# Second dense layers of a four-layer graph network with features on partitions

## The chip, the cores and the metric

The kernel runs on one core of a Trainium2 chip. The metric is the device time in microseconds of one execution. The kernel before takes 2306.15 us, the median of three runs between 2304.9 and 2306.2.

## The reference

32 graphs of 512 nodes with 256 features each pass through four layers. Every layer multiplies by the graph's own dense 512x512 adjacency matrix, adds the layer's input and normalises over the features. All arithmetic is float32.

```python
x = layernorm(x + relu(((1 + eps) * x + adj @ x) @ W1 + b1) @ W2 + b2)      # layer 0, hidden 512
h = adj @ (x @ W.T + b);  x = layernorm(x + where(h > 0, h, alpha * h))     # layer 1
h = layernorm(x);  x = layernorm(x + relu((adj @ h) @ W_rel + b_rel + h @ W_root) + x)   # layer 2
h = silu(rmsnorm((eps * x + adj @ x) @ W1 + b1))                            # layer 3, hidden 1024
x = layernorm(x + h @ W2 + b2)
```

(In layer 2 the layer's own result already contains x once.)

## The kernel before, in words

A graph is held as x in "token" layout: 128 partitions, on each of them four nodes (chunks c) with 256 features. SBUF has 36 buffers of 4 KB a partition ("rooms", line 639), PSUM its 8 banks, and there are 11 small tiles (`SMALL`, line 612).

Each large product is done with seven block products in place of eight (Strassen's scheme in Winograd's form). `seven` (line 764) calls `product` for m1 to m7 on three banks, and `take` or `put` to bring a bank into SBUF; `right_sums` and `weight_sums` make the sums of blocks that the seven products need. `aggregate` (line 880) gives adj @ x with features on partitions. `dense_feat` (line 920) is the first dense layer: weights are the stationary operand, 256 nodes the moving one, and hidden features stand on partitions. `dense_add` (line 963) is the second dense layer: nodes are the stationary operand, 128 columns of weights the moving one, and the product comes out in token layout. All seven `take` and `put` there are VectorE additions of a bank and a block of x, 128x256 elements. The bias of layers 0 and 3 has been added to x before, by `plus_row` (line 1138), two VectorE additions of 128x512. `done(j)` then starts the sums of the norm for half of the nodes.

Layer 2 needs its input with features on partitions too. `turned` (line 1092) does this in graphs 0 and 31 (`alone()`, line 628) with TensorE transposes, and in the others with two VectorE transposes, which turn each 32x32 square in place, and sixteen transfers within SBUF (`carry`) that put the squares where they belong.

The norm is class `Norm` (line 1015). It sums on ScalarE, one pass for the mean and one for the squares. `NormOnVector` (line 1079) takes VectorE's statistics. `layer3` (line 1219) uses the latter in graphs 0 and 31. The last graph (`b == B - 1`) ends its norm by halves of the nodes and stores each half (`finish`, line 1049); others are scaled and stored whole.

No engine's order is that of the program text. Every operation is recorded first (`Plan.add`), with the engines that can do it and an estimated duration. `order` (line 423) then plays the program through: at each step it takes the engine and operation that can start earliest, and among those that can start at about the same time the lowest rank. The rank is the graph's number times `period`, plus the TensorE work of its graph ahead of the operation times `pace`; the last three graphs (`LATE`) are spaced by `last` in place of `period`. `FLIGHT` allows five graphs at once, and rooms are kept back for older graphs. An operation that ScalarE or VectorE can do goes to VectorE only where this ends earlier by more than `YIELD`. `best` (line 417) plays each of the `RULES` and takes the one whose last operation starts earliest. The engines then get this order, fixed; each works through its own list and waits for the others through semaphores. All transfers are issued by SyncE, whose list is in the same order. Where GpSimd's power and a VectorE operation would meet, short VectorE memsets (`pause`, line 1316) keep them apart.

Of the kernel before, what the change touches and what calls it, by code (L numbers as in the profile page):

```python
# [14 lines left out]
P = 128  # L15
Q = 32
# [15 lines left out]
def matmul_time(n):  # L32
    return (0.224 if n <= 128 else 0.432), 0.163
# [47 lines left out]

TWO_OPERANDS = ("tensor_add", "tensor_sub", "tensor_mul", "scalar_tensor_tensor")
PORT = 0.55

# [1 line left out]
SOON = 0.03  # L88


YIELD = 0.8

# [2 lines left out]

RULES = [(48, 2, 8, 0.7), (48, 2, 20, 0.5), (45, 2, 12, 0.7)]  # L100

AHEAD, LAST = 70.0, 500.0


class Pool:
# [62 lines left out]
class Part:  # L170
# [10 lines left out]
    def __getitem__(self, i):  # L181
        return self.then(lambda v: v[i])

    def shaped(self, *shape):

        n = 1
        for d in shape:
            n *= d
        names = "abcd"[: len(shape)]
        kw = dict(zip(names, shape))  # L190
        return self.then(
            lambda v: v[:, 0:n].rearrange(f"p ({' '.join(names)}) -> p {' '.join(names)}", **kw)
        )
# [38 lines left out]
class Plan:  # L232
# [190 lines left out]
    def order(self, period, pace, last, near):  # L423

        final = max(op.graph for op in self.ops) - LATE
        need = self.needs(pace, near)
        rank = [
            (min(op.graph, final) * period + max(op.graph - final, 0) * last + n, i)
            for i, (op, n) in enumerate(zip(self.ops, need))
        ]  # L430
        tensor = sorted(r for r, op in zip(rank, self.ops) if "tensor" in op.ways)
# [14 lines left out]
        port = dict.fromkeys(free, 0.0)  # L446
        powers = {i for i, op in enumerate(self.ops) if op.port and "gpsimd" in op.ways}
        can_start = {i for i, n in enumerate(behind) if not n}
        crossed = False
        done = []  # L450
        while can_start:
            while oldest in left and not left[oldest]:
# [71 lines left out]
            op = self.ops[i]  # L524
            op.start, op.way = t, engine
            busy, tail = op.ways[engine][0]
            if engine == "tensor" and t > free[engine] + 0.01:
                busy += AGAIN
            if engine == "vector":
                crossed = op.crosses  # L530
                if crossed:
# [43 lines left out]
def tile_gnn_stack(ctx: ExitStack, tc: tile.TileContext, a: dict, out: bass.AP):  # L575
# [33 lines left out]
    HC = NC // 2  # L609
    TH = N // 2  # L610
    FH = FC3 // 2
    FLIGHT, ROOMS, SMALL = 5, 36, 11

    const = ctx.enter_context(tc.tile_pool(name="const", bufs=1))
    work = ctx.enter_context(tc.tile_pool(name="work", bufs=1))
# [6 lines left out]
        [  # L622
            memory.tile([P, 2, 2, P], F32, tag=f"diagonal{i}", name=f"diagonal{i}")
            for i in range(FLIGHT)
        ]
    )

# [15 lines left out]
    def vector(method, n, *args, **kw):  # L643
        return "vector", method, vector_time(n), args, kw
# [4 lines left out]

    def mm(o, lhsT, rhs, first, last):  # L650
        kw = dict(start=first, stop=last, skip_group_check=True)
        way = "tensor", "matmul", matmul_time(rhs.shape[-1]), (lhsT, rhs), kw
        plan.do(o, way, ordered=o.room)

    def flip(o, x):
# [29 lines left out]
    def carry(o, x):  # L685
        plan.move(o, x, o.shape[0] * span(o) / 256, late=1.2)
# [11 lines left out]
    def short(*shape):  # L698
        return Part(Room(rooms, whole=False)).shaped(*shape)
# [4 lines left out]
    def bank(*shape):  # L704
        return Part(Room(banks)).shaped(*shape)
# [22 lines left out]
    def constant(name, shape):  # L728
        return const.tile(shape, F32, tag=name, name=name)
# [27 lines left out]
    nc.vector.memset(scraps[0], 0.0)  # L757
    nc.vector.memset(mhalf, -0.5)
    pause = constant("pause", [P, 48])
    for tile_of_few in smalls.tiles:  # L760
        nc.vector.memset(tile_of_few, 0.0)

# [27 lines left out]
    def right_sums(b11, b12, b21, b22, t, t3):  # L790

        sub(t[0], b12, b11)
        sub(t[1], b22, t[0])
        sub(t3, b22, b12)
        sub(t[2], b21, t[1])
        return dict(m1=b11, m2=b21, m3=b22, m4=t[2], m5=t[0], m6=t[1], m7=t3)
# [123 lines left out]
    def dense_feat(aT, left, bias, hT, done):  # L920
# [6 lines left out]
        for f0 in range(0, n, 2):  # L927
# [21 lines left out]

            seven(*(bank(2, TH) for _ in range(3)), product, take, put)  # L950

    def dense_sums(upper, lower):


        right = {}
        for pairs in zip(upper, lower):
            blocks = [x[:, :, j * TH : (j + 1) * TH] for x in pairs for j in range(2)]
            sums = right_sums(*blocks, [short(2, TH) for _ in range(3)], blocks[1])
            for m, x in sums.items():
                right.setdefault(m, []).extend(x[:, e, :] for e in range(2))  # L960
        return right

    def dense_add(x, right, left, done):


        def block(i, j):
            return x[:, j * HC : (j + 1) * HC, i * P : (i + 1) * P]

        def product(m, ps, first):
            n = len(right[m])  # L970
            for k in range(n):
                for i in range(HC):
                    mm(
                        ps[:, i, :], right[m][k][:, i * P : (i + 1) * P], left[m][:, k, :],
                        first and i == 0 and k == 0, k == n - 1,
                    )

        def take(ps, i, j):
            add(block(i, j), ps, block(i, j))

        def put(ps, i, j, more):
            take(ps, i, j)
            if i == 1:
                done(j)

        seven(*(bank(HC, P) for _ in range(3)), product, take, put)

    def column_sums(t):

# [99 lines left out]
            ts(self.less[:, mine], means[:, mine, 0], -1.0, None, ALU.mult)  # L1089
            self.squares, self.n = means[:, :, 1], 1  # L1090

    def turned(h):

        hT = Wide(DC)
        if alone():
            for k in range(DC):
                ps = bank(N)
                for c in range(NC):
                    flip(ps[:, c * P : (c + 1) * P], h[:, c, k * P : (k + 1) * P])
                copy(hT.chunk(k), ps)  # L1100
        else:
            squares = Wide(DC)
            for k in range(DC):
                o = squares.chunk(k)
                plan.do(o, vector("transpose", N, h[:, :, k * P : (k + 1) * P]))
            places = [slice(q * Q, (q + 1) * Q) for q in range(P // Q)]
            to, of = (
                x.pair(0).then(lambda v: v.rearrange("p k (c i) -> p (k c) i", i=P))
                for x in (hT, squares)
            )  # L1110
            for p in places:
                for q in places:
                    carry(to[p, :, q], of[q, :, p])
        return hT

    def everywhere(sums, ops):

# [47 lines left out]
    def layer0(x, adjacency):  # L1165
        adjacency.sums()
        adjacency.with_loops(loop0)
        aT = aggregate(x, adjacency)
        adjacency.restore()
        plus_row(x, b2_0)  # L1170
        h1 = Wide(FC0)
        dense_feat(aT, A1_0, b1_0, h1, lambda f: act(h1.pair(f), h1.pair(f), AF.Relu))
        norm = Norm(x)
        dense_add(x, dense_sums(h1.rooms[:1], h1.rooms[1:]), A2_0, norm.half)
        norm.scales((1.0, LN_EPS))
        return norm.scaled()

# [26 lines left out]
    def layer2(h, xx, u, adjacency):  # L1204

        aT = aggregate(h, adjacency)
        hT = turned(h)
        norm = Norm(xx)

        def done(h):  # L1210
            stt(half(xx, h), half(u, h), 0.0, half(xx, h), ALU.max, ALU.add)
            norm.half(h)

        dense_add(u, dense_sums(hT.rooms, [aT]), A_2, done)
        adjacency.with_loops(loop3)
        norm.scales((1.0, LN_EPS))
        return norm.scaled()

    def layer3(x, adjacency, b):

        aT = aggregate(x, adjacency)
        plus_row(x, b2_3)
        hT, acc = Wide(FC3), short(N)

        def squares(f):
            sq = room(2, N)
            act(sq, hT.pair(f), AF.Square)
            if f == 0:
                add(acc, sq[:, 0, :], sq[:, 1, :])
            else:  # L1230
                add(acc, acc, sq[:, 0, :])
                add(acc, acc, sq[:, 1, :])

        dense_feat(aT, A1_3, b1_3, hT, squares)
        pr = everywhere(column_sums(acc), (1.0 / HID3, RMS_EPS, ALU.mult, ALU.add))
        right = {}
        for q in range(0, FH, 2):
            for f in (q, q + 1, FH + q, FH + q + 1):
                mul(hT.chunk(f), hT.chunk(f), pr)
                act(hT.chunk(f), hT.chunk(f), AF.Silu, scale=w_3[:, f : f + 1])  # L1240
            for m, t in dense_sums([hT.pair(q)], [hT.pair(FH + q)]).items():
                right[m] = right.get(m, []) + t
        norm = (NormOnVector if alone() else Norm)(x)
        place = out[b].rearrange("(p c) d -> p c d", c=NC)
        if b < B - 1:
            dense_add(x, right, A2_3, norm.half)
            norm.scales((1.0, LN_EPS))
            y = norm.scaled()
            plan.move(place, y, N * D / 256, into=f"out{b}")
        else:  # L1250

            def done(h):
                norm.half(h)
                norm.finish(h, 1.0, LN_EPS, half(place, h))

            dense_add(x, right, A2_3, done)
# [17 lines left out]
    A1_0 = weight_sums("A1_0", *quarters(W1_0))  # L1274
    b1_0 = col("L0_gnn_b1")
    b2_0 = row("L0_gnn_b2")
    W2_0 = weight("L0_gnn_W2")
    A2_0 = weight_sums("A2_0", *blocks_of(W2_0[:, 0:2], W2_0[:, 2:]))
    alpha = row("L1_gnn_alpha")
# [17 lines left out]
    b1_3 = col("L3_gnn_b1")  # L1297
    w_3 = col("L3_gnn_rms_weight")
    b2_3 = row("L3_gnn_b2")
    eps3 = row("L3_gnn_epsilon")  # L1300
    loop3 = constant("loop3", [P, P])
    ts(loop3, ident, eps3, None, ALU.mult)
# [52 lines left out]
```

## Time and profile before

| | |
|---|---|
| median of three runs | 2306.15 us |
| the profiled execution | 2307.14 us, its span 2305.4 us |
| TensorE busy | 2286.7 us, 99% |
| weight loads busy | 2094.1 us, 91% |
| VectorE busy | 2167.7 us, 94% |
| ScalarE busy | 1583.2 us, 69% |
| GpSimd busy | 239.7 us, 10% |
| moved by DMA | 122.84 MB, 53 GB/s |

Busy is the time in which an engine runs at least one instruction. TensorE's matmuls overlap one another, so its busy time says that it has work, and not how fast this passes; the time from one start to the next says that. The chain is the work that ended last, followed back from the end. Almost every instruction has line 317 (the helper that issues), so groups are told apart by the tiles that they write and read: `ps` is a PSUM bank, `room` an SBUF buffer, `A` sums of weights, `L_gnn_W` weights, `few` a small tile, `line` and `diagonal` memory in DRAM.

### The profile page before, as it was taken

What the parts mean: (1) busy time and instruction counts of PE and PEld (TensorE: products, weight loads), DVE (VectorE), ACT (ScalarE), POOL (GpSimd) and SP (SyncE); (2) the same over time, 40 slices, a digit from 0 to 9 for tenths busy, and PEclk for the clock granted to TensorE, in tenths of its full rate; (3) what the DMA queues carried; (4) which work ended last, traced back from release to release, by engine and by line L of the source; (5) the groups of instructions that cost most, each with busy time, mean ns of one, the idle gap of its engine ahead of it and who ended that gap; (6) DMA issues with size and microseconds to landing.
All of it is one profiled execution on the core that took longest, in us unless ns stands there. A gap on an engine that the chain in (4) does not pass through costs nothing.

```text
span 2305.4 us, 41217 instructions
## 1 busy us (share of the span) xinstructions
PE 2286.7 (99%) x14002; PEld 2094.1 (91%) x14002; DVE 2167.7 (94%) x5556; ACT 1583.2 (69%) x4338; POOL 239.7 (10%) x167
## 2 busy tenths in 40 slices
PE   9999999999999999999999999999999999999998
PEld 8899999999999999999999999999999999999888
DVE  8999999999999999999999999999999999979898
ACT  4766767667677677676676766767767767676576
POOL 0001110111010111101111011110011110111101
PEclk9999999999999999999999999999999999999999
DMA  6112221122211222121221112221222212201101
GB/s 190 46 41 64 53 68 24 51 65 61 53 31 55 61 64 59 26 55 57 65 60 35 49 52 64 60 60 24 56 60 65 60 24 55 70 10 38 51 6 42
DMA packets 223747, 122.84 MB, mean 53 GB/s; under 512 B 142896, under 2 KB 194352, under 8 KB 223536
## 3 DMA queue, kind: packets, MB, share of 16 engines
q1 hardware_dynamic: 223536, 120.20, 19.2%
q8 instruction: 111, 1.82, 0.3%
q14 instruction: 100, 0.82, 0.1%
HBM read 78.92 MB, written 24.97 MB: 45 GB/s over the span
## 4 chain that ended last, share of the span: by engine, by line
PE 95%; DVE 2%; ACT 1%; DMA 1%; SPq 0%; issue 0%; ACTq 0%; DVEq 0%
PE ps L317 95%; DVE room L317 2%; ACT room L317 1%; DMA room<-in_adj_dram 1%; ACT scrap L317 0%; DMA L_gnn_W<-in_L_gnn_W_dram 0%; SPq L357 0%; DMA room<-line 0%; DVE few L317 0%; DVE few L336 0%; DVE A L317 0%; DVE pause L1316 0%; DVE L_gnn_W_root L317 0%; DVE L_gnn_W L317 0%; DVE L_gnn_W_rel L317 0%
## 5 line engine op out<-in xcount | busy, mean ns | idle before, releaser
L317 PE MATMUL ps<-room,room 128*128 128x256 f32 x3584 | 908.8, 381 | 1.6 <-DVE room L317 0.8
L317 DVE TENSOR_TENSOR room<-room,room 128x512 f32<-128x512 f32 (+1 forms) x1360 | 772.4, 595 | 14.6 <-ACT room L317 8.2
L317 PEld LDWEIGHTS ps<-room,room 128*128 128x128 f32 x3584 | 639.9, 191 | 75.6 <-DVE room L317 5.6
L317 DVE TENSOR_TENSOR room<-ps,room 128x256 f32<-128x256 f32 (+1 forms) x1344 | 611.2, 473 | 60.3 <-PE ps L317 42.9
L317 PE MATMUL ps<-L_gnn_W,room 128*128 128x128 f32 (+1 forms) x3584 | 600.6, 290 | 1.3 <-ACT room L317 0.8
L317 PEld LDWEIGHTS ps<-L_gnn_W,room 128*128 128x128 f32 x3584 | 525.7, 191 | 32.7 <-ACT room L317 1.8
L317 PE MATMUL ps<-A,room 128*128 128x128 f32 x3072 | 457.9, 275 | 0.0
L317 POOL TENSOR_TENSOR few<-few,mhalf 128x4 f32<-128x4 f32 (+3 forms) x161 | 239.0, 1485 | 2060.0 <-DVE few L317 1944.3
L317 PEld LDWEIGHTS ps<-A,room 128*128 128x128 f32 x3072 | 426.5, 191 | 18.9 <-DVE room L317 0.4
L317 PE MATMUL ps<-room,L_gnn_W 128*128 128x256 f32 x1536 | 400.4, 379 | 1.9 <-DVE room L317 1.9
L317 ACT ACTIVATE room<-ps,L_gnn_b_c 128x256 f32<-128x256 f32 x768 | 318.2, 475 | 70.9 <-PE ps L317 67.1
L317 ACT ACTIVATE room<-ps 128x256 f32<-128x256 f32 x509 | 186.4, 383 | 252.1 <-PE ps L317 248.9
L317 ACT ACTIVATE room<-room 128x1024 f32<-128x1024 f32 (+2 forms) x260 | 242.3, 944 | 132.6 <-DVE room L317 86.5
L317 ACT ACTIVATE scrap<-room 128x256 f32<-128x256 f32 x504 | 206.5, 411 | 170.2 <-DVE room L317 141.2
L317 PEld LDWEIGHTS ps<-room,L_gnn_W 128*128 128x128 f32 x1536 | 282.7, 190 | 38.5 <-DVE room L317 2.8
L317 DVE TENSOR_TENSOR room<-room 128x256 f32<-128x256 f32 (+1 forms) x640 | 311.7, 495 | 5.3 <-ACT room L317 2.1
L317 ACT ACTIVATE room<-room,few 128x256 f32<-128x256 f32 x525 | 286.4, 593 | 33.4 <-DVE few L317 33.3
L317 PE MATMUL ps<-room,A 128*128 128x256 f32 x1152 | 305.6, 381 | 3.0 <-ACT room L317 3.0
L317 ACT ACTIVATE scrap<-room,few 128x256 f32<-128x256 f32 x504 | 251.2, 502 | 20.1 <-DVE few L317 19.0
L317 PEld LDWEIGHTS ps<-room,A 128*128 128x128 f32 x1152 | 209.9, 191 | 31.7 <-ACT room L317 3.9
L317 ACT ACTIVATE room<-room,L_gnn_rms_weight_c 128x512 f32<-128x512 f32 x256 | 176.0, 714 | 33.2 <-DVE room L317 33.0
L317 DVE TENSOR_TENSOR room<-room,loop 128x256 f32<-128x256 f32 x256 | 103.8, 416 | 18.3 <-PE ps L317 15.8
(59 smaller groups left out, 1198.7 us busy)
## 6 DMA issues: line engine op xcount, KB each, us to landing
room<-in_adj_dram SPq DMA_DIRECT2D x128, 256.0 KB, 5.0
room<-in_x_dram SPq DMA_DIRECT2D x31, 512.0 KB, 5.9
out_dram<-room SPq DMA_DIRECT2D x31, 512.0 KB, 2.9
room<-room SPq DMA_DIRECT2D x480, 32.0 KB, 2.0
diagonal<-room SPq DMA_DIRECT2D x62, 128.0 KB, 1.8
room<-in_adj_dram SPq DMA_DIRECT2D x124, 64.0 KB, 2.0
room<-diagonal SPq DMA_DIRECT2D x62, 128.0 KB, 2.3
room<-line SPq DMA_DIRECT2D x30, 256.0 KB, 3.3
```

The costliest lines, as they stand in the source:

```text
L317: getattr(getattr(self.nc, engine), method)(to, *(put(x) for x in args), **kw)
```

## The change

1. `dense_turned` takes the place of `dense_add` in layers 0 and 3 of graphs 1 to 28 (`TURN`). Weights are now the stationary operand and 256 nodes the moving one, so features stand on partitions. Four of the seven results are brought to SBUF by ScalarE, which adds the bias; three are VectorE additions. Two VectorE transposes turn the 32x32 squares, `spread_squares` writes them to DRAM in four transfers and reads them back in one, and `add_turned` adds the result to x by halves. `plus_row` is left out there.
2. In layer 2 the sixteen transfers of `turned` become four into DRAM and four back (`gather_squares`). `dense_add` itself stays in layer 2, and in layers 0 and 3 of graphs 0 and 29 to 31.
3. The last two graphs (`HALVES`) take VectorE's statistics in the final norm, and end and store it by halves.
4. The planner has one rule (37, 2, 19, 0.6) in place of three, shifts for the ranks of the set-up, of graph 1 and of the last two graphs, `YIELD` 1.2 for 0.8, `AHEAD` 50 for 70, and a model of a TensorE that runs at half speed for a while after an idle time (`COLD`). `SMALL` is 10.
5. A Silu of one column ahead of all work makes ScalarE load its table then. Two bias columns are loaded besides.

```diff
-RULES = [(48, 2, 8, 0.7), (48, 2, 20, 0.5), (45, 2, 12, 0.7)]
-AHEAD, LAST = 70.0, 500.0
+RULES = [(37, 2, 19, 0.6)]
+SHIFT = {-1: -12, -2: 6, 1: -6}
+AHEAD, LAST = 50.0, 500.0
+TURN = {0: (0, 3), 2: (99, 0), 3: (0, 3)}
+HALVES = 2
...
+                if idle > COLD[0]:
+                    cold = t + COLD[1]
+                if cold - COLD[2] < t < cold:
+                    busy *= 2
...
-    FLIGHT, ROOMS, SMALL = 5, 36, 11
+    FLIGHT, ROOMS, SMALL = 5, 36, 10
...
+    nc.scalar.activation(pause[:, 0:1], pause[:, 0:1], AF.Silu)
...
+    def turns(layer):
+        return TURN[layer][0] < plan.graph < B - TURN[layer][1]
...
+    def dense_turned(right, left, bias=None):
+        yT = Wide(DC)
+        def product(m, ps, first):
+            n = len(right[m])
+            ps = ps.then(lambda v: v.rearrange("p (c a j) -> p c a j", c=HC, j=Q))
+            for k in range(n):
+                mm(ps, left[m][:, k, :], right[m][k], first and k == 0, k == n - 1)
+        def block(i, j):
+            return yT.chunk(i)[:, j * TH : (j + 1) * TH]
+        def take(ps, i, j):
+            if bias is None:
+                copy(block(i, j), ps)
+            else:
+                act(block(i, j), ps, AF.Identity, bias=bias[:, i : i + 1])
+        def put(ps, i, j, more):
+            if more:
+                add(block(i, j), ps, block(i, j))
+            else:
+                take(ps, i, j)
+        seven(*(bank(TH) for _ in range(3)), product, take, put)
+        squares = room(P // Q, NC, DC, Q)
+        for k in range(DC):
+            plan.do(
+                squares.then(lambda v: v.rearrange("p b c k j -> p k c b j"))[:, k],
+                vector(
+                    "transpose", N,
+                    yT.chunk(k).then(lambda v: v.rearrange("p (c b j) -> p c b j", c=NC, j=Q)),
+                ),
+            )
+        y = spread_squares(squares)
+        return y.whole(P // Q, NC, DC, Q).then(lambda v: v.rearrange("p a c k j -> p c k a j"))
+
+    def add_turned(x, y, done):
+        x = x.then(lambda v: v.rearrange("p c (k a j) -> p c k a j", k=DC, j=Q))
+        for h in range(2):
+            add(half(x, h), half(x, h), half(y, h))
+            done(h)
...
+    def spread_squares(of):
+        to = room(P // Q, NC * DC * Q)
+        of, via = of.whole(P // Q, NC * DC * Q), next(corners)
+        names = [f"{via.tensor.name}{a}" for a in range(P // Q)]
+        places = via.rearrange("(b i) (a x) -> a i b x", i=Q, a=P // Q)
+        for a, name in enumerate(names):
+            plan.move(places[a], of[a * Q : (a + 1) * Q], Q * N * DC / 256, into=name)
+        plan.move(to.whole(N * DC), via, P * N * DC / 256, late=0.8, outof=names)
+        return to
+
+    def gather_squares(to, of):
+        to, of, via = to.whole(N * DC), of.whole(N * DC // Q, Q), next(corners)
+        names = [f"{via.tensor.name}{a}" for a in range(P // Q)]
+        via = via.rearrange("(i b) x -> i (b x)", i=Q)
+        places = via.rearrange("i (m a j) -> a i m j", a=P // Q, j=Q)
+        for a, name in enumerate(names):
+            plan.move(places[a], of[a * Q : (a + 1) * Q], Q * N * DC / 256, into=name)
+        blocks = via.rearrange("i (b x) -> b i x", b=P // Q)
+        for b in range(P // Q):
+            plan.move(to[b * Q : (b + 1) * Q], blocks[b], Q * N * DC / 256, late=0.8, outof=names)
...
+        if turn:
+            add_turned(x, dense_turned(right, A2_0, b2c_0), norm.half)
+        else:
+            dense_add(x, right, A2_0, norm.half)
...
-        norm = (NormOnVector if alone() else Norm)(x)
+        norm = (NormOnVector if b == 0 or b >= B - HALVES else Norm)(x)
-        if b < B - 1:
-            dense_add(x, right, A2_3, norm.half)
+        if b < B - HALVES:
+            if turn:
+                add_turned(x, dense_turned(right, A2_3, b2c_3), norm.half)
+            else:
+                dense_add(x, right, A2_3, norm.half)
```

## The prediction

> **What bounds the kernel now.** I read the busy line and the chain of the page first, then the chain in order of time, then the busy times by stretch, then the instructions of TensorE (PE) in order of time.
>
> ```profile
> PE 2286.7 (99%) x14002; PEld 2094.1 (91%) x14002; DVE 2167.7 (94%) x5556; ACT 1583.2 (69%) x4338; POOL 239.7 (10%) x167
> ...
> PE 95%; DVE 2%; ACT 1%; DMA 1%; SPq 0%; issue 0%; ACTq 0%; DVEq 0%
> ```
>
> PE is busy for 99% of the span and makes up 95% of the chain that ended last. VectorE (DVE) is close behind, so both must be watched. A busy PE is not yet a PE at its rate, hence the next two views: the chain in time (start, length), and the stretch from 500 to 1000 us (length, then busy time and instructions of PE, weight loads, DVE, ACT, POOL, then clock, DMA share, GB/s).
>
> ```profile
> 62.35 2010.53 PE ps L317 x12322
> ```
>
> ```profile
> 500.00:1000.00 500.00, 500.00 (x3078) 458.66 (x3078) 474.25 (x1208) 347.46 (x963) 54.26 (x36) 1.00 0.20 53
> ```
>
> From 62 to 2073 us the chain is one unbroken piece of PE. In the stretch PE never idles at full clock, DVE is busy 474.25 of 500 (95%), ACT 347.5 (69%). What does one matmul instruction cost there? Each f32 product of the program stands in the trace as two MATMUL records ("passes"). Start to start in the timeline:
>
> ```profile
> 1031.68 2.75 PE L317 MATMUL ps<-room,room 128*128 128x256 f32 x12
> 1034.28 1.03 PE L317 MATMUL ps<-room,L_gnn_W 128*128 128x256 f32 x4
> 1035.14 1.03 PE L317 MATMUL ps<-room,A 128*128 128x256 f32 x4
> ...
> 2267.07 4.18 PE L317 MATMUL ps<-L_gnn_W,room 128*128 128x128 f32 x36
> ...
> 2271.09 0.61 PE L317 MATMUL ps<-A,room 128*128 128x128 f32 x4
> ```
>
> Twelve passes of 256 columns take 1034.28 - 1031.68 = 2.60 us, 0.2167 each; four of the first dense layer 0.86 us, 0.215 each. Thirty-six of 128 columns take 4.02 us, 0.1117 each. Over all starts between 100 and 2050 us the means are 0.1115 (128) and 0.2160 (256, first dense layers) to 0.2173 (256, aggregations). A graph has 106 products of 256 columns and 112 of 128: 212 x 0.2162 + 224 x 0.1115 = 70.8 us. The saved diagonals show the real period:
>
> ```profile
> 1004.46 0.96 SPq L357 DMA_DIRECT2D diagonal<-room  x2
> ...
> 1075.34 0.96 SPq L357 DMA_DIRECT2D diagonal<-room  x2
> ```
>
> 1075.34 - 1004.46 = 70.88 us. So in the middle only the number and width of the matmuls count; some 4 us in 2010 are anything else. The ends are different. Where each stretch is set against its passes at these rates, PE loses 8.9 us until its first product, 5.6 us from there to 62 us, 7.7 us from 2073 to 2293 us, and runs out of work at 2295.7, 9.7 us ahead of the end.
>
> **What the skill says of it.** The Trainium skill, page TensorE: Matmul & The Clock Gate, section Back-to-back issue gap, gives a matmul N/2.4 + 2.5 ns: a fixed part for each instruction, so that one wide one is cheaper than two narrow ones. The trace agrees in kind. If a f32 pass of N columns counts as 2N, the rule gives 109.2 and 215.8 ns, the trace 111.5 and 216.0. The saving for two passes made one is 2.5 ns by the rule and 7.0 by the trace; the forecast goes by the trace, because the change lives on just this difference. For the transfers, DMA: Bandwidth & Descriptors, Specifications, asks for at least 512 B in a piece. The trace has 142896 packets under 512 B, and the 32 KB transfers that are made of them land after 2.0 us, as late as a 128 KB diagonal (1.8). The new transfers of layers 0 and 3 have pieces of 1 KB and 4 KB; I price them by the diagonal and line rows.
>
> **The change part by part**, against the profiled execution (2307.1 us, span 2305.4).
>
> *Matmuls, layers 0 and 3.* 28 + 56 products of 128 columns become 14 + 28 of 256. Per graph 42 x (4 x 0.1115 - 2 x 0.2160) = 42 x 0.014 = 0.59 us. This holds in graphs 1 to 28 (layer 2 stays): 28 x 0.59 = 16.5 us, all of it on the path. Bounds: with 0.2173 for the wide pass 14.3 us at least, with a rounded 0.112 19 at most. Weight loads halve there; they were behind PE anyway.
>
> *DVE, per turned layer.* Gone: two row additions of the bias (684 ns) and four of seven additions out of PSUM (416 ns), 3.03 us. New: two transposes of 128x512 (690) and two additions of 128x512 (682), 2.74 us. So -0.29 us, twice a graph: 67.2 becomes 66.7 us in a period of 70.3, 95% as before. The new operands come in runs of 32 elements. No row has just these; steps of 4 elements (158 ns for 32x4) and diagonal blocks of 128 (416 ns, as contiguous ones) cost nothing extra, so I take none. The upper bound, twice the time, would be 5.5 us a graph and is in the rivals.
>
> *ACT.* Four evictions with bias at 475 ns per turned layer: +3.8 us on about 49 per graph, 76% of the period. ACT's longest waits are for PE already, and that free time covers them; were it gone, a bank would come free half a us later and PE would wait for it. The higher penalty for vector (1.2 for 0.8) moves some of the 115 scalings at 406 ns from DVE to ACT (593). Both nothing on the path.
>
> *Transfers.* Per turned layer four writes of 128 KB (about 0.45 us issue each, landing 1.8 as the diagonal) and a read of 512 KB. The line row has 256 KB in 3.3 us, the prefetched x 512 KB in 5.9; I take 4 to 5. With transposes and issues the sum is 10 us of latency, twice a graph. It lies beside other graphs' matmuls. The addition of y is what waits; behind it on DVE, which works in order, are other graphs' evictions, and PE waits for their banks. Layer 2's sixteen transfers (about 0.65 us issue each, 10.4 in sum) become four and four, some 8 us for 12. SyncE has then 34 issues for 32 a graph, with waits for writes in between; adjacency and x loads queue behind these, but land well ahead of use now. Bytes go from 3.5 to 6 MB a graph, the DMA share from 0.20 to some 0.3. I charge 0.8 us in all; bounds 0 and the rival below.
>
> *End.* The last graph's final norm is as before. The one before takes DVE statistics (four of 406 and four of 174 ns, 2.3 us, in DVE's idle time there) and halves in place of eight ACT sums and their reads:
>
> ```profile
> 2299.55 1.01 ACT room L317 x2
> ...
> 2300.61 0.60 ACT room L317
> 2301.20 0.49 ACTq L1351
> ```
>
> That graph's last store goes out at 2301.7, the last graph's own at 2300.7; with the former early the end follows the latter: -1.1 us. The new ranks (period 37 and 19 at the end, shifts, half clock in the planner's costs) can save part of the 7.7 us lost from 2073 on, of which 3 is this wait and some 2.5 the half clock after it:
>
> ```profile
> 2204.91 1.72 PE L317 MATMUL ps<-room,A 128*128 128x256 f32 x4 [2.98 <-ACT room L317]
> ```
>
> It can also add as much, since more graphs meet at the end. Bounds -7.7 and +8; I take -3.0.
>
> *Start.* The table load (1.28 us at 5.10) goes ahead of the first data, where ACT idles. DVE waited 1.3 us for the copies behind it, but PE's first product waited for x, which lands at 8.8. I take -0.7, bounds -2 and +2. One small buffer of eleven fewer costs nothing: the waits show none for these. Two small bias columns add about 1 us of SyncE issue, covered by loads under way.
>
> Sum: -16.5 + 0.8 - 1.1 - 3.0 - 0.7 = -20.5 us, 2286.6 in the profiled execution's terms. The median of the runs is 1.0 lower than that execution: 2285.6.
>
> **Rivals.**
> 1. *The gain is half eaten.* A turned layer holds up to a room more until its transposes, and 36 rooms with about 3.8 graphs under way (2 x 71 / 37) are fewer than ten each; loads or banks come late and PE idles 0.2 to 0.5 us a graph, or the ends get 5 to 8 us worse. 2285.6 + 7 to 17: 2292 to 2303. For: DVE has only 5% free. Against: 4 us of loss in 2010 now.
> 2. *Slower: DVE is stopped by the addition of y.* If y lands later than the order written ahead of time allows, DVE stands at that addition. Its free time is 70.3 - 66.7 = 3.6 us a graph. From there on each us is PE's, and above 3.6 + 0.73 us (20.5 / 28) the change loses. At 5.5 us, 2.7 for each of two waits: 1.9 x 28 = 53 us, about 2339. Runs of 32 at double time come to the same. For: in-order engine, no margin seen for a 512 KB read. Against: DVE waited just 1.4 us in all for the line transfers, which are of this kind.
> 3. *The change does nothing in the middle*: a turned pass costs 0.2195 and the wide form saves nothing beyond 4 x 0.1115 - 2 x 0.2195 = 0.007, half. Then 2294, inside rival 1. The first dense layers at 0.2160 speak against it.
>
> **How the numbers follow.** The main case has 0.66, its own range 2277 to 2293; rivals 1 and 3 together 0.23; rival 2 0.11, reaching from 2306 to 2345. The likeliest gives 2285.6. A range from 2277 to 2301 leaves out rival 2, the upper edge of rival 1 and a little below. A measurement of this kernel can tell about 0.2%, 4.6 us, from no change: faster (below 2301.5) 0.66 + 0.19 = 0.85, within 0.04, slower 0.11.
>
> **What would show it.** Right: a period of 70.3 us between the saved diagonals; twice as many ACT evictions with bias less some; PE without idle time in the middle; DVE near 95%. Wrong: DVE or PE waits on a transfer named room<-corner, passes of a turned layer above 0.216, or PE idle beyond 16 us at the ends.

## The result and the profile after

The kernel takes 2336.89 us after the change (median of 4 runs, 2330.42 to 2340.77) and 2306.18 before, on the same chip. The ratio is 1.0131, 95% interval 1.0118 to 1.0143: the change costs 30.7 us, where I had forecast a gain of 20.5. The profiled execution is 2338.3 us, its span 2336.5.

The page first, its busy line and the chain that ended last by engine:

```profile
PE 2283.9 (98%) x11650; PEld 2014.7 (86%) x11650; DVE 2134.7 (91%) x5390; ACT 1696.2 (73%) x4600; POOL 239.7 (10%) x168
...
PE 29%; DVE 3%; DMA 3%; ACT 1%; issue 0%; SPq 0%; ACTq 0%; POOLq 0%; POOL 0%; DVEq 0%
```

PE has its 2352 passes fewer and is still busy for nearly the whole span, but it is no more the chain: 29% in place of 95% (the walk back stops at 1464 us, so the shares do not add up to all). VectorE (DVE) is less busy than before, not more. The same stretch from 500 to 1000 us (columns as before the change: length, then busy time of PE, weight loads, DVE, ACT, POOL, then clock, DMA share, GB/s):

```profile
500.00:1000.00 500.00, 492.42 (x2442) 432.34 (x2442) 459.77 (x1154) 371.18 (x1014) 52.82 (x35) 1.00 0.31 89
```

PE was busy for all 500 us there; now 7.6 are missing, at full clock. DVE has fallen from 474 to 460, which is 66.3 us in a period of 72.06 where I had forecast 66.7: it does no more work than forecast, and waits in between. The period between the saved diagonals, forecast at 70.3 us:

```profile
1065.87 0.98 SPq L372 DMA_DIRECT2D diagonal<-room  x2
...
1137.67 0.98 SPq L372 DMA_DIRECT2D diagonal<-room  x2
```

That is 71.80 us here. The mean over twenty graphs (7 to 27) is 72.06, and was 70.93 before. Where each graph loses it, the chain in order of time shows (start, length, what):

```profile
1559.80 6.45 DMA room<-corner
...
1566.27 0.70 DVE room L332
...
1567.00 0.91 ACT scrap L332 x4
1567.90 1.00 ACT room L332 x3
...
1568.95 65.15 PE ps L332 x326
```

Before, one piece of PE reached from 62 to 2073 us. Now it breaks once per graph: a transfer out of `corner`, the DRAM memory that the new transfers go through, then one DVE addition, then ScalarE's (ACT's) statistics and evictions, then PE again for 65 us. The timeline of another such place, from 1119 to 1138 us (start, length, engine, operation; in brackets how long the engine had been idle, and for what):

```profile
1120.31 5.30 SPq L372 DMA_DIRECT2D corner<-room  x8
...
1125.85 2.24 SPq L372 DMA_DIRECT2D room<-corner  x5
...
1133.47 1.29 DVE L332 TENSOR_TENSOR room<-room,room 128x512 f32<-128x512 f32 x2 [1.78 <-DMA room<-corner]
1134.20 0.42 ACT L332 ACTIVATE scrap<-room 128x256 f32<-128x256 f32 x1 [2.02 <-DVE room L332]
...
1136.16 1.13 PE L332 MATMUL ps<-room,room 128*128 128x256 f32 x4 [1.05 <-ACT room L332]
```

SyncE issues eight writes in one go, four of y of one graph and four of layer 2 of another, then four reads of layer 2 and the read of y. The addition of y (`add_turned`, 128x512) starts 1.78 us late; ACT has been waiting 2.02 us for it; the evictions behind that come late and PE stands 1.05 us. The waits of the whole run (total, times, longest):

```profile
DVE room L332 <- DMA room<-corner: 48.0, 43, 3.0
...
PEld ps L332 <- ACT room L332: 41.7, 43, 2.5
...
PE ps L332 <- ACT room L332: 26.8, 28, 2.1
```

By tiles, 29.9 of the 48.0 us stand before additions of y and 18.0 before the 128x512 additions that sum layer 2's transposed h. The page's last part, the DMA issues (count, KB each, median us from issue to landing):

```profile
corner<-room SPq DMA_DIRECT2D x344, 128.0 KB, 2.5
room<-in_adj_dram SPq DMA_DIRECT2D x128, 256.0 KB, 6.4
room<-corner SPq DMA_DIRECT2D x56, 512.0 KB, 3.7
...
out_dram<-room SPq DMA_DIRECT2D x30, 512.0 KB, 6.5
```

`x56` is the read of y. Its 3.7 us hides two kinds: the one that meets nothing lands after 3.5 us (median), the one among layer 2's transfers after 5.72. The order counts on 4.43. The output, which is issued 0.44 us (median) behind the second kind, took 2.9 us before and takes 6.5 now; a block of adjacency 5.0 and 6.4.

One measure is used below: PE's lost time from 300 to 2000 us, that is 1700 us less its passes in that stretch at 0.2162 us (256 columns) and 0.1113 (128). It is 3.1 us before and 43.0 after. The same loss outside the stretch, at the two ends, is 29.5 before and 35.7 after. At these rates the passes themselves take 15.0 us less, so the bill is 40 + 6.2 - 15.0, the 31.2 us between the two profiled spans. The planner's own timetable, the starts that it worked out when it wrote the order, had the last operation at 2296.9 us before and 2279.3 after. Before, the chip stays 2.6 to 2.8 us behind it from 1000 to 2060 us; after, it is 30 us behind at 1066 us and 53 at 2086, 1.7 to 1.8 us more with every graph.

### The profile page after: what moved, and what is told of

It reads as the page before. It is cut to its first block, busy times and chain, and to the rows that moved or that the text cites. A ratio compares the mean times of both kernels' runs of the same rounds, so it can differ in the third digit from the quotient of the medians.

```text
span 2336.5 us, 36619 instructions
## 1 busy us (share of the span) xinstructions
PE 2283.9 (98%) x11650; PEld 2014.7 (86%) x11650; DVE 2134.7 (91%) x5390; ACT 1696.2 (73%) x4600; POOL 239.7 (10%) x168
## 5 line engine op out<-in xcount | busy, mean ns | idle before, releaser
L332 PE MATMUL ps<-room,L_gnn_W 128*128 128x256 f32 x2880 | 764.6, 380 | 5.4 <-DVE room L332 5.1
L332 PEld LDWEIGHTS ps<-room,L_gnn_W 128*128 128x128 f32 x2880 | 537.3, 190 | 83.4 <-DVE room L332 12.1
L332 PE MATMUL ps<-room,A 128*128 128x256 f32 x2160 | 577.4, 379 | 1.3 <-ACT room L332 1.3
L332 ACT ACTIVATE room<-ps,L_gnn_b_c 128x256 f32<-128x256 f32 x992 | 408.9, 468 | 125.2 <-PE ps L332 123.4
L332 PEld LDWEIGHTS ps<-room,A 128*128 128x128 f32 x2160 | 407.7, 190 | 55.4 <-ACT room L332 2.0
L332 PE MATMUL ps<-L_gnn_W,room 128*128 128x256 f32 (+1 forms) x896 | 201.3, 336 | 3.3 <-DVE room L332 1.7
L332 PEld LDWEIGHTS ps<-L_gnn_W,room 128*128 128x128 f32 x896 | 150.1, 191 | 20.3 <-DVE room L332 2.2
L332 PE MATMUL ps<-A,room 128*128 128x128 f32 x1056 | 143.0, 276 | 0.0
L332 PEld LDWEIGHTS ps<-A,room 128*128 128x128 f32 x1056 | 136.1, 192 | 4.9 <-DVE room L332 0.3
L332 DVE STREAM_TRANSPOSE room<-room 128x512 f32<-128x512 f32 x172 | 115.2, 693 | 0.8
```

The lines of the kernel that those rows point to most:

```text
L332: getattr(getattr(self.nc, engine), method)(to, *(put(x) for x in args), **kw)
```

## The experiments

Two theories. **Y**: y lands later than the fixed order counts on, and DVE, ACT and PE queue behind it (my rival 2). Within Y, the question is what makes y late: its own way through DRAM, or the crowd of layer 2's small pieces. **O/G**: the new order, or `gather_squares`, costs the time by itself, and the wait for y is only where it shows. The first six kernels but the fourth keep the order of every engine's instructions as it is in the kernel after the change, so that only the edit differs.

**1. No transfers of y.** The four writes and the read of both turned layers are not issued; the additions add what is in the buffer. So y is left out of the result.

```diff
+            if left_out:
+                return
...
-            plan.move(places[a], of[a * Q : (a + 1) * Q], Q * N * DC / 256, into=name)
-        plan.move(to.whole(N * DC), via, P * N * DC / 256, late=0.8, outof=names)
+            plan.move(places[a], of[a * Q : (a + 1) * Q], Q * N * DC / 256, into=name, left_out=True)
+        plan.move(to.whole(N * DC), via, P * N * DC / 256, late=0.8, outof=names, left_out=True)
```

> The changed kernel with every engine's order kept, but the five transfers of each turned layer (four writes, one read of 512 KB) are not issued; the addition reads whatever its buffer holds, so the results of layers 0 and 3 lack the second dense product. Theory Y (y lands later than the fixed order allows, the addition of y stops VectorE, ScalarE's sums stand behind it and TensorE waits for ScalarE): TensorE's waits of 1 to 2.5 us a graph go, the period falls from 71.8 to about 70.3 us, the time to 2283 to 2292. Theory G (layer 2's eight small-piece transfers and their late landing are what hurts): stays above 2320. Theory O (the new order with more graphs under way is itself the loss): stays within 5 us of 2337.

Measured: 2292.39 us (2291.51 to 2294.22), ratio 0.9939 (0.9925 to 0.9954). PE's loss falls from 43.0 to 3.1 us, DVE's waits on `corner` from 40.8 to 2.5 in that stretch, the period to 70.26. It is a little above the range given, but far from what O/G asked for: without y's transfers the order and `gather_squares` lose no more in that stretch than the kernel before.

**2. No transfers of layer 2.** The eight transfers of `gather_squares` are not issued; layer 2 works with what the buffer holds.

```diff
-            plan.move(places[a], of[a * Q : (a + 1) * Q], Q * N * DC / 256, into=name)
+            plan.move(places[a], of[a * Q : (a + 1) * Q], Q * N * DC / 256, into=name, left_out=True)
...
-            plan.move(to[b * Q : (b + 1) * Q], blocks[b], Q * N * DC / 256, late=0.8, outof=names)
+            plan.move(to[b * Q : (b + 1) * Q], blocks[b], Q * N * DC / 256, late=0.8, outof=names, left_out=True)
```

> The changed kernel with every engine's order kept, but layer 2's eight transfers are not issued; layer 2 of graphs 1 to 30 then works with stale values for the turned h. Theory Y with a collision (y is late because layer 2's transfers are issued just ahead of it, at 0.6 to 0.7 us each, and share the DMA engines): most of the loss goes, 2285 to 2305. Theory Y without a collision (y's read is too slow by itself, at 3.2 to 3.7 us): within 8 us of 2337. Theory O: within 5 us of 2337.

Measured: 2286.09 us (2285.54 to 2286.78), ratio 0.9911 (0.9896 to 0.9926), period 70.10. All transfers of y are there, and from 300 to 2000 us DVE waits just 0.4 us for them. The chain in order of time:

```profile
126.10 1905.24 PE ps L332 x9630
```

PE is one piece again, for 1905 us. So y alone is in time, and layer 2 alone (experiment 1) is harmless: the loss comes of the two together. This is the time that I had forecast for the whole change, reached with layer 2's transfers gone.

**3. The read of y twice.** A dose upward, order kept: the read is issued a second time into the same buffer.

```diff
-            getattr(self.nc, engine).dma_start(to, of, **kw)
+            for _ in range(times):
+                getattr(self.nc, engine).dma_start(to, of, **kw)
...
-        plan.move(to.whole(N * DC), via, P * N * DC / 256, late=0.8, outof=names)
+        plan.move(to.whole(N * DC), via, P * N * DC / 256, late=0.8, outof=names, times=2)
```

> The changed kernel with every engine's order kept, but the 512 KB read of y is issued twice, one after the other, into the same buffer; the result is the same. Theory Y: y lands 1.3 to 2 us later; in the crowded place all of it is lost (28 x 1.3 to 2 = 36 to 56 us), at the other, where y has some 1.2 us to spare, up to 0.8 us more a graph: 2370 to 2415. Theory O: no more than 10 us above 2337.

Measured: 2516.32 us (2510.48 to 2518.25), ratio 1.0905 (1.0889 to 1.0921), period 78.60. The dose was larger than meant: the second read was not issued beside the first but only when that had landed (at 1218.86 us for 1214.93), so y came 3.9 us later (mean) and not 1.3 to 2. The waits from 300 to 2000 us:

```profile
DVE room L332 <- DMA room<-corner: 152.4, 46, 5.2
PEld ps L332 <- ACT room L332: 136.4, 98, 5.1
PE ps L332 <- ACT room L332: 103.8, 40, 4.7
```

Two reads per graph, 3.9 us each, are 7.8 us of lateness; the period grew by 78.60 - 72.06 = 6.5, some 0.84 us per us. Not all of this is waiting. The next lines are the stretch from 300 to 2000 us after the change and here; the clock, third from the right, is 1.00 and 0.97:

```profile
300.00:2000.00 1700.00, 1670.96 (x8291) 1468.41 (x8289) 1558.56 (x3900) 1258.22 (x3425) 176.34 (x117) 1.00 0.31 88
```

```profile
300.00:2000.00 1700.00, 1578.69 (x7603) 1368.27 (x7602) 1431.20 (x3586) 1159.13 (x3146) 162.67 (x109) 0.97 0.32 93
```

By the trace's clock records PE had half its clock for 85 us of this stretch, against 3 after the change. My estimate from these is 41 us of work lost to the clock, 1.9 a graph, which leaves 4.6 us for 7.8, some 0.6 us of waiting per us of lateness. So this addition has little slack, though not none.

**4. Layer 2's new transfers without turned layers.** `dense_add` everywhere, `gather_squares` kept, ranks (with shifts and `AHEAD`) searched anew for this program.

```diff
-TURN = {0: (0, 3), 2: (99, 0), 3: (0, 3)}
+TURN = {0: (99, 0), 2: (99, 0), 3: (99, 0)}
...
-RULES = [(37, 2, 19, 0.6)]
+RULES = [(35, 2, 8, 0.7)]
```

> The changed kernel with no layer turned: dense_add in layers 0 and 3 everywhere, layer 2's eight transfers kept, and ranks (35, 2, 8, 0.7; shifts -6, 0, -12; AHEAD 60) with which the program's own plan ends at 2300 for the 2297 of the kernel before. Theory Y: the plan holds as it does in the kernel before (4 to 8 us over it), about 2304 to 2312. Theory O (deep interleaving loses on the chip whatever is interleaved) or theory G: the chip slips against the plan by 1 us or more a graph, 2330 or more.

Measured: 2326.37 us (2325.47 to 2328.91), ratio 1.0088 (1.0071 to 1.0105). It fell between the two expectations. This order had a worse plan to begin with (2300.1 us), and slips from it by some 0.5 us a graph; PE loses 15.6 us. The wait is now one line:

```profile
DVE room L332 <- DMA room<-corner: 11.1, 9, 1.9
```

With no y in the program this is layer 2's own read, late against its own margin. So my sharp form of Y, "only y suffers", is too narrow: a transfer that the order waits for closely can come late with no y about.

**5. Layer 2 written in large pieces.** Order kept, same bytes, same eight transfers; the writes put down rows of 1 KB in place of 1024 pieces of 128 bytes. The blocks then stand in other places, so layer 2 gets a permuted h.

```diff
+        lines_of = of.then(lambda v: v.rearrange("p m j -> p (m j)"))
-        places = via.rearrange("i (m a j) -> a i m j", a=P // Q, j=Q)
+        pieces = via.rearrange("(b i) (a x) -> a i b x", i=Q, a=P // Q)
...
-            plan.move(places[a], of[a * Q : (a + 1) * Q], Q * N * DC / 256, into=name)
+            plan.move(pieces[a], lines_of[a * Q : (a + 1) * Q], Q * N * DC / 256, into=name)
```

> The changed kernel with every engine's order kept and all transfers issued, but layer 2's four writes go to DRAM in pieces of 1 KB in place of 128 B (same bytes, other places, so layer 2's turned h is permuted wrongly). Theory P (the small pieces are what delays: 0.56 to 0.70 us of issue each for the 0.45 planned, and a long landing): the loss goes for the most part, 2286 to 2300. Theory B (it is the bytes and the number of transfers in the crowded 12 us): at most a third of the 50 us goes, 2320 to 2337.

**6. Layer 2 written, but not read back.** Order kept; the four reads of `gather_squares` are not issued, so layer 2 works with what the buffer holds.

```diff
-            plan.move(to[b * Q : (b + 1) * Q], blocks[b], Q * N * DC / 256, late=0.8, outof=names)
+            plan.move(to[b * Q : (b + 1) * Q], blocks[b], Q * N * DC / 256, late=0.8, outof=names, left_out=True)
```

> The changed kernel with every engine's order kept, but of layer 2's eight transfers the four reads are not issued, the four small-piece writes are (layer 2 takes stale values for the turned h). Theory P: the writes are still there, so at least half of the loss stays, 2312 to 2337. Theory B: half of the bytes ahead of y are gone and SyncE is freed of four issues, so more than half goes, 2286 to 2312.

Measured: 2297.62 us (2296.25 to 2299.77), ratio 0.9962 (0.9948 to 0.9976), with large pieces (number 5); 2297.61 (2296.99 to 2302.22), ratio 0.9965 (0.9952 to 0.9978), without the reads (number 6). The first was expected, the second was not, if the small pieces were all of it: either half of the crowd, taken away, brings back 39 us. Both fit if the parts add up against a margin, and only what their sum exceeds it by is lost. Medians for the y among the crowd, from 300 to 2000 us:

| | issue after the crowd's first write | landing after its issue | landed after the first write | PE lost |
|---|---|---|---|---|
| planned | 5.96 | 4.43 | 10.39 | |
| after the change | 7.07 | 5.72 | 13.08 | 43.0 |
| 5, large pieces | 5.88 | 4.95 | 11.03 | 8.1 |
| 6, no reads | 6.90 | 4.48 | 11.59 | 12.1 |

At 2.7 us behind plan the loss is 43 us; at 0.6 to 1.2 it is 8 to 12. Small pieces make y late in two ways. A write of 1024 pieces of 128 bytes takes SyncE 0.68 us to issue (planned 0.45), one of 128 pieces of 1 KB 0.44. And y then lands 5.72 us after its own issue, in place of 4.95 with large pieces (where the output also follows it 1 us later, 1.48 for 0.44). The small pieces themselves land in 2.7 us, hardly later than the large ones (2.3).

The small pieces are but a part of the crowd. Right behind y, SyncE issues the output, four blocks of adjacency and as a rule the next x. In the kernel after the change 2048 KB of these (median) are issued before y lands, and the mean busy share of the 16 DMA engines is 0.90 while y is under way; at the y that meets nothing it is 0.49. In experiment 3 this traffic waits for the second read. There the first read, with layer 2's eight transfers ahead of it as ever, lands after 4.28 us in place of 5.72: a transfer is also held up by what is issued behind it. The output shows the same from the other side. It lands after 6.5 us in the kernel after the change and after 3.1 in experiment 1, where the small pieces and their reads stand ahead of it as before and only y's transfers are missing. So the small pieces hold up what follows together with y, not by themselves.

The Trainium skill, page DMA: Bandwidth & Descriptors, section Why small descriptors are slow (HBM only), says that transfers from SBUF to SBUF do not suffer the penalty of small pieces that those with DRAM do. No run here settles this. In number 8 below the same 128-byte pieces go from SBUF to SBUF in sixteen transfers, and the output right behind them lands in 3.1 us; but so it does in experiment 1, behind pieces that go to DRAM. How the pieces hold up y, these runs do not show.

**7. The planner told of the issue and of y.** Nothing of the work is changed; 0.66 us of SyncE for a small-piece write, y 2.0 us later, ranks (with shifts, `YIELD` and `AHEAD`) searched anew.

```diff
-        plan.move(to.whole(N * DC), via, P * N * DC / 256, late=0.8, outof=names)
+        plan.move(to.whole(N * DC), via, P * N * DC / 256, late=2.8, outof=names)
...
-            plan.move(places[a], of[a * Q : (a + 1) * Q], Q * N * DC / 256, into=name)
+            plan.move(places[a], of[a * Q : (a + 1) * Q], Q * N * DC / 256, into=name, small=True)
```

> Nothing of the work changed; the planner is told what the chip showed: issue 0.66 us for the small-piece writes, and y landing 2.0 us later than before (late 2.8 for 0.8). The order is made anew with ranks (38, 2, 18, 0.4), shifts -18, 0, -3, YIELD 0.9, AHEAD 55, with which the program's own plan ends at 2280.8 (2279.3 in the changed kernel, 2296.9 in the one before). Theory Y: with the lateness planned for, the additions of y come when it is there; the chip keeps to the plan within 4 to 10 us, 2286 to 2294, faster than both kernels. Theory O (or a bandwidth limit that no order escapes): slips by 1 us a graph again, above 2315.

Measured: 2327.03 us (2324.55 to 2328.26), ratio 1.0087 (1.0072 to 1.0102): a miss. The DVE additions that sum layer 2's h, by tile and shape (count, busy, mean ns, then the idle time ahead and what ended it):

```profile
L332 DVE TENSOR_TENSOR room<-room 128x512 f32<-128x512 f32 x144 | 99.1, 689 | 51.4 <-ACT room L332 27.1 <-DMA room<-corner 18.5 <-DMA room<-in_adj_dram 5.5
```

All 18.5 us that DVE waits for `corner` from 300 to 2000 us now stand here: the wait has moved from y, whose margin was mended, to layer 2's reads, whose margin was not. The chip is 35 us behind this plan at 1984 us.

**8, 9, 10. Two by two.** Layer 2 as in the change or with its sixteen transfers from SBUF to SBUF as before; the planner with its durations or with those of the traces. Layers 0 and 3 are turned in all. Each program has ranks (for 8 and 10 with `YIELD` and `AHEAD`) searched for it anew, to plans that end within 4.2 us of one another (2279.1 to 2283.3).

```diff
+                for p in places:
+                    for q in places:
+                        carry(to[p, :, q], of[q, :, p])
-                gather_squares(hT.pair(0), squares)
...
-        plan.move(to.whole(N * DC), via, P * N * DC / 256, late=0.8, outof=names)
+        plan.move(to.whole(N * DC), via, P * N * DC / 256, late=2.5, outof=names)
...
-                plan.move(chunk, a["adj"][b][:, m, :], P * N / 256, late=1.6)
+                plan.move(chunk, a["adj"][b][:, m, :], P * N / 256, late=3.6)
...
-            plan.move(x, src, N * D / 256, late=1.6)
+            plan.move(x, src, N * D / 256, late=3.0)
```

The diff is number 8. Number 9 keeps `gather_squares`, with 0.66 us for its writes' issue, `late=2.4` for its reads and 2.8 for y; number 10 has the carries and the old durations.

> Layers 0 and 3 are turned as in the kernel after the change, but layer 2's blocks again go from SBUF to SBUF in sixteen transfers, as before; the planner is told 1.7 us more for the landing of y, 2.0 more for adjacency and 1.4 more for x, and the order is planned anew (its own plan ends at 2282.1 us by the last start). Lateness theory (what was lost is only that transfers land later than the fixed order counts on, and small pieces through DRAM make that crowd): no DVE wait on y above 5 us in all in 300 to 2000 us, period 70.1 to 70.6 us, 2284 to 2296 us, so ahead of both kernels. Rival (reading y back through DRAM is by itself more than the order can bear, whatever layer 2 does): DVE again waits some 1 to 2 us per graph on y, 2310 us or more.

> The work of the kernel after the change, unchanged; the planner is told the durations that the traces show: 0.66 us of SP for a write in small pieces, 2.0 us more for the landing of y, 1.6 more for layer 2's reads, 2.0 more for adjacency and 1.4 for x, and the order is planned anew (its own plan ends at 2283.3 us). Lateness theory: with every margin right, the waits on y and on layer 2's reads go below 5 us in all in 300 to 2000 us, 2286 to 2298 us. Rival (the crowd of small pieces delays some transfer whatever is planned): DVE waits move to another transfer again, as when only y and the issue were told, 2310 us or more.

> The fourth corner of two by two: layer 2's sixteen transfers from SBUF to SBUF as before, and the planner's durations left as the kernel after the change has them (y 0.8 us late, adjacency and x 1.6); only the ranks are searched anew, to a plan that ends at 2279.1 us, against 2279.3 of the kernel after the change. Theory C (the crowd of layer 2's small pieces is the cause, and the margins were enough for layers 0 and 3 alone): y lands as planned, no DVE wait on y above 10 us in all in 300 to 2000 us, 2284 to 2296 us. Theory M (the margins are the cause, and telling them is what helped): the order has y late again, DVE waits 0.5 to 1.5 us a graph on y or on adjacency, 2300 to 2330 us.

| us, and ratio to before (95%) | durations as in the change | durations of the traces |
|---|---|---|
| `gather_squares` | 2336.89, 1.0131 (1.0118 to 1.0143), the change | 2301.04, 0.9981 (0.9972 to 0.9990), number 9 |
| sixteen carries | 2295.32, 0.9957 (0.9941 to 0.9974), number 10 | **2290.03, 0.9934 (0.9917 to 0.9950)**, number 8 |

Number 8 is faster than both kernels, by 16 us and by 47. Number 10, whose plan ends where that of the change does (2279.1 for 2279.3), shows that the old margins were nearly enough for y as long as layer 2 stays in SBUF and in this order. Number 9 came out 3 us above the range given for lateness, and far below the rival's 2310: with every margin told, this crowd can be borne. DVE's waits on `corner` from 300 to 2000 us, number 8, then 9, then 10:

```profile
DVE room L332 <- DMA room<-corner: 0.7, 2, 0.4
```

```profile
DVE room L332 <- DMA room<-corner: 0.7, 2, 0.4
```

```profile
DVE room L332 <- DMA room<-corner: 5.2, 9, 1.5
```

And number 8's busy line and two of its DMA rows:

```profile
PE 2268.0 (99%) x11650; PEld 2013.6 (88%) x11650; DVE 2124.5 (93%) x5373; ACT 1709.1 (75%) x4637; POOL 243.0 (11%) x168
...
room<-corner SPq DMA_DIRECT2D x56, 512.0 KB, 3.6
...
out_dram<-room SPq DMA_DIRECT2D x30, 512.0 KB, 3.1
```

The same kernel's timeline of SyncE shows that the output has the sixteen transfers right ahead of it:

```profile
1158.20 11.40 SPq L372 DMA_DIRECT2D room<-room  x16
1170.01 0.35 SPq L372 DMA_DIRECT2D out_dram<-room  x1
```

It lands about as before the change (median 3.1 us, for 6.5), and y lands in 3.6. But the last y was issued some 45 us before this output, where in the kernel after the change it was 0.44; in numbers 9 and 10 the distance is 48 and 45 (medians), and the next y comes 3 us after the output or later. So these three orders also keep y and the output apart, and what that is worth beside the change that each was made for, the two by two cannot tell. PE loses 0.7 us from 300 to 2000 in number 8, 8.4 in number 9; that 7.7 is most of the 8.7 us between their profiled spans (2288.4 and 2297.1). In number 9 the weight loads wait 8.1 us for DVE in 26 small pieces and 6.8 us in 21 for nothing that the profile shows; why its order leaves those is open. The verdict on the crowd rests on 1, 2, 5 and 6, where the order is fixed.

## Why the prediction was wrong

- **Matmuls, -16.5 us: right, and all of it was there.** In the profile after, passes of 256 columns take 0.216 us start to start and those of 128 0.112 (medians), within a nanosecond of the rates that I used; the count fell by 2352, from 14002 to 11650. Where nothing waits the period is 70.10 us (experiment 2) or 70.17 (number 8), for 70.3 forecast. Rival 3 (a turned pass at 0.2195) is out. One sum was off without effect: at 0.2173 the lower bound is 13.4 us, not 14.3. The formula that the prediction takes from the Trainium skill, page TensorE: Matmul & The Clock Gate, section Back-to-back issue gap, is given there for an isolated matmul and not for such streams; the forecast rightly went by the trace.
- **DVE and ACT: right.** DVE's transposes take 693 ns and the 128x512 additions, those with runs of 32 elements among them, 683 ns in the mean, for 682 before. Where nothing waits (experiment 2) DVE has 66.0 us of work in a graph, for 66.7 forecast.
- **Transfers, +0.8 us: this is the step that failed.** It said of layer 2, "Layer 2's sixteen transfers (about 0.65 us issue each, 10.4 in sum) become four and four, some 8 us for 12", and took this for relief; of y, "4 to 5" us. Alone y takes 3.5, so that estimate was safe. What was wrong is that I priced each group by itself, and layer 2's pieces by their number and not by where they go: I held the mark of 512 bytes that I had cited against layers 0 and 3, and not against the 128-byte pieces that layer 2 was now to write to DRAM. Together, y came 2.7 us behind plan once per graph, and this term measured 43.0 - 3.1 = 40 us from 300 to 2000 us alone, in place of 0.8.
- **"DVE waited just 1.4 us in all for the line transfers, which are of this kind": a false comfort.** The line transfers met no crowd: of their 24 reads from 300 to 2000 us before the change, 22 had no other transfer under way. Nor did I compare a landing with what the order allows for it (4.43 us after issue in the planner's terms).
- **The cushion, the second thing that failed.** My break-even for rival 2, 3.6 + 0.73 us per graph, took DVE's idle time as a cushion: 2.7 us of lateness in a graph should have cost nothing. It cost 40 us in some 23.6 graphs, 1.7 us each, which is 0.6 us per us, the share that experiment 3 leaves as well. DVE's idle time mostly lies elsewhere in the period, and ACT and PE wait in the meantime.
- **Rival 2 named the mechanism** (DVE stopped at the addition of y, evictions behind it, PE after them) and the view that would show it (`room<-corner`). That its price, 2339, comes within 2 us of the measured 2336.9 is luck: it assumed two late landings of 2.7 us in a graph with 3.6 us of them absorbed, and there was one, of which little was absorbed. Its chance, 0.11, was too small; the cause of the lateness it did not name.
- **Ends, -4.8 us in all: mostly not there.** PE's loss before 300 and after 2000 us is 29.5 us before, 28.0 in experiment 2, 29.9 in number 8 and 26.5 in number 10: between nothing and 3 us gained. In the kernel after the change it is 35.7, a loss of 6 more. In experiment 2 this miss is made up for by a middle better than forecast (a period 0.83 us shorter, for 0.59 forecast), so its 2286.1 agrees with my 2285.6 partly by luck.

## What to carry to other kernels

In a kernel whose engines follow an order written ahead, a transfer is priced as a margin: when it lands, with all that is issued around it, against when the order wants it; idle time of the waiting engine elsewhere in the period is a poor cushion (here some 0.6 of each us came through). Look for the place where two groups of transfers meet once per period, and price that place, not each group alone, with what is issued behind it too. Keep small pieces away from the last microseconds before a close wait; here the fastest kernel moved them within SBUF. And when a change alters what a transfer costs, give the planner the new durations of all transfers near it, since one mended margin moves the wait to the next.

## What the runs showed of the hardware

- A transfer's landing depends on what is issued around it, ahead and behind. The same 512 KB read of y lands after 3.5 us alone, after 4.3 with layer 2's eight transfers ahead of it (experiment 3), and after 5.7 when the output and adjacency follow right behind as well. The output, 0.44 us behind y, lands after 6.5 us; without y's transfers, and with all else as it was, after 3.1.
- Writes in pieces of 128 bytes lose little themselves (2.7 us for 2.3), while the read of y that follows them lands 0.8 us later than with pieces of 1 KB (5.72 for 4.95; with small pieces the output also follows y 1 us sooner, which may be a part of it).
- The issue of a 128 KB write takes SyncE 0.68 us in 1024 pieces of 128 bytes and 0.44 in 128 of 1 KB (medians of the profile after). The order counted on 0.45 for both.
